# Gathers of table rows: each issued only once the second one before it has landed

## The chip, the core and the metric

The kernel runs on one core of a Trainium2 chip. The metric is the device time of one execution in microseconds (us), as the median of several runs. The core has a matrix engine (PE, with weight loads shown apart as PEld), a vector engine (DVE), a scalar engine (ACT), a general engine (POOL, called GpSimd in the program) and SyncE (SP), whose queue issues most plain DMAs. Each engine works through its own instructions in order, and they wait for one another through semaphores.

## What is computed

Four graph attention layers over 3327 nodes with 512 features; the graph is a random 0/1 matrix `adj` of 3327 x 3327 in which a row holds a few tens of ones at most. Cut to what matters, one layer is:

```python
h = jnp.maximum(_layernorm(x, axis=-1), 0.0)
Wh = h @ W                                   # split into heads: 8, 4, 1 and 8 in the four layers
e = leaky_relu(s_src[:, None] + s_dst[None, :], 0.2)     # s_src, s_dst: Wh dotted with two vectors
e = where(adj > 0, e, -inf)
x = x + softmax(e, axis=1) @ Wh              # in layers 1 and 2 with an elu around the product
```

In layer 0 and 1 every node is its own neighbour as well.

## The kernel before

The kernel makes use of how few neighbours a node has. In a first stage (`tile_gat_stack`) it reads `adj`, finds the column numbers of the ones in each row, sorts the nodes by their number of neighbours, and keeps for each of 26 tiles of 128 nodes a list of neighbour numbers, `CAPS[t]` of them (36 in the first tile, down to 11 in the last). If any row had too many ones, a dense kernel (`tile_gat_dense`) would run instead; it does not with these inputs.

The four layers are in `tile_gat_lists`. A node's features, already multiplied by the layer's weights, stand as one row of 528 floats (2112 bytes) in a table in HBM: `tabs[0]` and `tabs[1]` in turn, and `tabx` for layer 0, whose rows are double (features and the input `x` side by side). For a tile of 128 nodes, gather number k reads the row of each node's k-th neighbour: 128 rows, one in each partition, 270,336 bytes. The helper `gather` (L833) issues it on POOL as an indirect DMA: POOL writes the descriptors, the sixteen DMA engines move the rows. A node's own row needs no list and comes by a plain DMA on SP (L865), except in layer 0.

The work of a layer is a list of steps. A step is a group of up to `GROUP = 4` neighbours of one tile; tiles go from the last (shortest lists) to the first. Three methods of `Tile` make up a step. `fetch` issues the group's gathers into a buffer of `gpool`. `scored` adds the scores (DVE, L887), bends them and takes the exponential (ACT, L890). `group` multiplies the rows by the weights (DVE, L918) and lets PE sum them in PSUM (L923); in layer 2, with one head, DVE multiplies and adds in one operation (L911). When a tile's last group is done, a chain of pieces ends it: divisors, means, normalisation, transposes, product with the next layer's weights (L468), scaling (L475), and a store of the new row into the next table (L995).

The order on each engine is written out by hand (`tc.manual_schedule`): the loop over s issues the fetch of steps up to s + `LOOK`, then the scores of step s + 1, then the products of step s, then the pieces that `later` has put at this step. `LOOK` is 7, and `gpool` has seven buffers:

```python
                while fetched < min(len(steps), s + LOOK):
                    steps[fetched][0].fetch()
                    fetched += 1
```

A fetch waits for nothing but a free buffer and, at the start of a layer, for the rows of the last tile of the layer before.

Nodes with very long lists would need many gathers, so the first `DENSE[l]` tiles of layers 1 to 3 (1, 9 and 3 tiles) are done densely, as masked products over all nodes (`Wholes` in layer 2, `Several` in layers 1 and 3). Their rows come by plain DMAs on SP. The masks for them are made in layer 0: `Mask` gathers nine tiles of whole rows of `adj` (L1022), and `Ranked` gathers 26 pieces from `found` (L1063). These use the same helper `gather`.

POOL also does a few other things in the layers: reciprocal roots in layer 2 (L431), additions of weights in layer 2 (L1139), and the scatters of the finished rows to the output (L842, called by `scatter`), which are indirect DMAs but do not go through `gather`.

Of the kernel before, what the change touches and what calls it, by code (L numbers as in the profile page):

```python
# [33 lines left out]
FAR = -30000.0  # L34
ROW = 528
GROUP = 4
DENSE = [0, 1, 9, 3]
ND = max(DENSE)
ROUND = 1.5 * 2.0 ** 23
# [455 lines left out]
class Slots:  # L495
# [5 lines left out]
    class Part:  # L501
        def __init__(self, pool, name, blocks):
            self.blocks, c = [], 0
            for t0, t1 in blocks:
                k = CAPS[t0] if t0 >= min(DENSE) else 1
                self.blocks.append((t0, t1, k, c))
# [17 lines left out]
def tile_gat_stack(ctx: ExitStack, tc: tile.TileContext, x, adj, adjT, ws, avs, out):  # L524
# [266 lines left out]
    with cond.Else():  # L791
        tile_gat_lists(tc, x, adj, ws, avs, out, ident, half, slots, L, low, spare, tabx, tabs)
# [3 lines left out]
def tile_gat_lists(ctx: ExitStack, tc: tile.TileContext, x, adj, ws, avs, out, ident, half, slots, L, low, spare, tabx, tabs):  # L796
# [7 lines left out]
    nc = tc.nc  # L804
# [25 lines left out]
    nc.vector.memset(zero, 0.0)  # L830
    L, low, spare = [t.rearrange("p a b -> p (a b)") for t in (L, low, spare)]

    def gather(out_, table, which):  # L833
        nc.gpsimd.indirect_dma_start(out=out_, out_offset=None, in_=table,  # L834
                                     in_offset=bass.IndirectOffsetOnAxis(ap=which, axis=0))

    waiting = []

# [6 lines left out]
    class Tile:  # L845


        def __init__(self, l, t, W):
            self.l, self.t, self.W = l, t, W

            first = GROUP - 1 if l == 0 else GROUP
            self.k0 = [0] + list(range(first, CAPS[t], GROUP))
            self.own = first - 1 if l == 0 else 0
            self.groups = []

        def fetch(self):

            l, t = self.l, self.t
            i = len(self.groups)
            k0 = self.k0[i]  # L860
            n = (self.k0 + [CAPS[t]])[i + 1] - k0
            g = gpool.tile([P, GROUP, ROW], F32, name="g")
            for q in range(n):
                if l > 0 and k0 + q == 0:
                    nc.sync.dma_start(g[:, 0, :], tabs[l % 2][t * P:(t + 1) * P, :])  # L865
                elif l > 0:
                    gather(g[:, q, :], tabs[l % 2], slots(t, k0 + q))
                elif k0 + q == self.own:
                    gather(g[:, q:q + 2, :].rearrange("p q n -> p (q n)"), tabx, slots(t, 0))
                else:  # L870
                    gather(g[:, q, :], tabx.rearrange("r (s n) -> (r s) n", s=2),
                           slots(t, k0 + q + (k0 == 0), twice=True))
            self.groups.append((k0, n, g))

        def scored(self, i):
# [4 lines left out]
            if i == 0:  # L880
# [4 lines left out]
                nc.vector.tensor_copy(self.s, g[:, n, F:F + H] if self.l == 0 else g[:, 0, F // 2:F // 2 + H])  # L885
            z = small.tile([P, GROUP, 8], F32, name="z")[:, :n, :H]
            nc.vector.tensor_tensor(z, g[:, :n, ROW - 8:ROW - 8 + H],  # L887
# [9 lines left out]
        def group(self, i):  # L897


            H, K, wt = HEADS[self.l], CAPS[self.t], self.wt  # L900
            D = F // H
            k0, n, g = self.groups[i]
            if H == 1:
                for q in range(n):
                    v = g[:, q, :].rearrange("p (s m) -> p s m", s=2)[:, :, :F // 2]
                    acc = self.po.rearrange("p (s m) -> p s m", s=2)
                    w = wt[:, k0 + q, 0:1]
                    if k0 + q == 0:
                        nc.vector.tensor_scalar(acc, v, w, None, OP.mult)
                    else:  # L910
                        nc.vector.scalar_tensor_tensor(acc, v, w, acc, OP.mult, OP.add)  # L911
                return
            m = pools["m"].tile([P, GROUP, F], F32, name="m")
            for q in range(n):
                v = g[:, q, :].rearrange("p (s m) -> p s m", s=2)[:, :, :F // 2]

                out_ = self.po if k0 + q == 0 else m[:, q, :]
                nc.vector.tensor_tensor(out_.rearrange("p (s h d) -> p s h d", s=2, d=D),  # L918
                                        v.rearrange("p s (h d) -> p s h d", d=D),
                                        wt[:, k0 + q, :H].rearrange("p (s h) -> p s h", s=2)  # L920
                                        .unsqueeze(3).to_broadcast([P, 2, H // 2, D]), OP.mult)
            for q in range(k0 == 0, n):
                nc.tensor.matmul(self.po, ident, m[:, q, :], start=False, stop=(k0 + q == K - 1),  # L923
                                 skip_group_check=True)
# [89 lines left out]
    class Mask:  # L1014
# [12 lines left out]
        def group(self, i):  # L1027
            self.m = pools["m"].tile([P, GROUP, F], F32, name="m").rearrange("p q n -> p (q n)").bitcast(BF16)[:, :NP]
            nc.scalar.activation(self.m, self.a, AF.Copy)
# [310 lines left out]
    at = {}  # L1340
# [11 lines left out]
    for l in range(NL):  # L1352
# [3 lines left out]
        with ExitStack() as c2:  # L1356
            def pool(name, bufs, **kw):
                return c2.enter_context(tc.tile_pool(name=f"{name}{l}", bufs=bufs, **kw))
# [10 lines left out]
            else:  # L1369
                pools.update(m=pool("mpool", 3))  # L1370
                pools.update(p=pool("ps_p", 1 if DENSE[l] else 2, **psum))
                if DENSE[l]:
                    pools.update(w=pool("ps_w", l // 3 + 1, **psum), r=pool("ps_r", 1, **psum))
                    if DENSE[l] > 1:
                        pools.update(e=pool("epool", 1))
                    wholes = Several(l, DENSE[l], W)
                    pw = pools["p"].tile([P, BANK], F32, name="pw")
# [91 lines left out]
```

## Time and profile before

| what | value |
|---|---|
| median of three runs | 2429.07 us (2425.39 to 2435.29) |
| span of the profiled execution | 2971.7 us |
| first gather of layer 0 issued | 273.7 us |
| stretch of gathers in layer 0, 1, 2, 3 | 777, 690, 419, 629 us |
| gathers through the helper | 1511 |
| busy share of PE, DVE, POOL, ACT | 74%, 65%, 58%, 31% |
| POOL's time for one gather (issue) | 0.95 us |
| DMA: bytes moved, rate over the span | 594.21 MB, 200 GB/s |
| share of 16 DMA engines: software queue, SP's queue | 49.8%, 16.4% |

The profile comes from one execution, and that execution is longer than the runs: its span, from the first instruction to the last, is 2971.7 us, against a median of 2429.07 us. The profile gives no time of that execution other than its span. A busy time is the time in which an engine worked. In a row of waits the engine and line that waited stand ahead of the arrow, and what released them behind it. A gather's row on POOL shows the time in which POOL wrote descriptors; when the rows are in place is told by a semaphore, and can be read from what waits for it and from the records of single DMA packets.

### The profile page before, as it was taken

What the parts mean: (1) busy time and instruction counts of PE and PEld (TensorE: products, weight loads), DVE (VectorE), ACT (ScalarE), POOL (GpSimd) and SP (SyncE); (2) the same over time, 40 slices, a digit from 0 to 9 for tenths busy, and PEclk for the clock granted to TensorE, in tenths of its full rate; (3) what the DMA queues carried; (4) which work ended last, traced back from release to release, by engine and by line L of the source; (5) the groups of instructions that cost most, each with busy time, mean ns of one, the idle gap of its engine ahead of it and who ended that gap; (6) DMA issues with size and microseconds to landing.
All of it is one profiled execution on the core that took longest, in us unless ns stands there. A gap on an engine that the chain in (4) does not pass through costs nothing.

```text
span 2971.7 us, 27155 instructions
## 1 busy us (share of the span) xinstructions
PE 2211.9 (74%) x7082; PEld 1246.1 (42%) x7082; DVE 1923.1 (65%) x4968; ACT 934.6 (31%) x2502; POOL 1731.4 (58%) x1717
## 2 busy tenths in 40 slices
PE   4777677776777764767777877588696688878887
PEld 2564233343433332434444444244354454545443
DVE  7987666655565533656665665598888366666665
ACT  5872122322221111322222322244333333323330
POOL 7885455565566635544556562676664556555653
PEclk9988888888898887988888898799898898989888
DMA  6885576786676756755667673787785566656663
GB/s 230 325 291 161 165 228 200 211 254 207 195 225 197 199 130 200 200 157 174 187 190 210 179 209 92 234 255 240 241 246 153 168 193 204 185 170 198 195 189 111
DMA packets 260731, 594.21 MB, mean 200 GB/s; under 512 B 103699, under 2 KB 121107, under 8 KB 256214
## 3 DMA queue, kind: packets, MB, share of 16 engines
q0 software_dynamic: 124368, 432.13, 49.8%
q1 hardware_dynamic: 132454, 153.45, 16.4%
q10 hardware_dynamic: 3744, 6.82, 0.7%
q8 instruction: 57, 0.93, 0.1%
q14 instruction: 108, 0.88, 0.1%
HBM read 542.60 MB, written 49.65 MB: 199 GB/s over the span
## 4 chain that ended last, share of the span: by engine, by line
PE 24%; DVE 18%; issue 14%; another core or an unknown queue 8%; ACT 5%; POOL 3%; DMA 2%; SPq 0%; DVEq 0%; POOLq 0%; ACTq 0%
PE bank L923 16%; DVE m L918 6%; PE pv L468 4%; PE whole L1301 3%; DVE bank L911 3%; POOL g L834 3%; ACT r L1267 1%; DVE z L889 1%; DVE z L887 1%; DVE x L961 1%; PE whole L1153 1%; DMA g<-tab,idxb 1%; DVE em L1126 1%; DVE q L438 1%
## 5 line engine op out<-in xcount | busy, mean ns | idle before, releaser
L923 PE MATMUL bank<-m,ident 128*128 128x512 f32 x2414 | 1232.2, 659 | 335.9 <-DVE m L918 197.3
L918 DVE TENSOR_TENSOR m<-g,pw 128x512 f32<-128x512 f32 x1207 | 752.5, 682 | 384.1 <-ACT pw L890 209.2
L834 POOL DMA_INDIRECT g<-tab,idxb x712 | 678.8, 953 | 482.0 <-issue 197.1
L923 PEld LDWEIGHTS bank<-m,ident 128*128 128x128 f32 x2414 | 488.8, 211 | 942.1 <-issue 582.4
L468 PE MATMUL pv<-w,hT 128*128 128x264 f32 x1664 | 434.9, 416 | 87.8 <-ACT hT L457 61.8
L834 POOL DMA_INDIRECT g<-tabx,twiceb x342 | 324.8, 950 | 230.7 <-issue 147.7
L834 POOL DMA_INDIRECT g<-tab,idxa x297 | 283.7, 955 | 248.4 <-issue 83.9
L468 PEld LDWEIGHTS pv<-w,hT 128*128 128x128 f32 x1664 | 334.1, 205 | 190.3 <-ACT hT L457 68.7
L890 ACT ACTIVATE pw<-z 128x32 f32<-128x32 f32 (+4 forms) x356 | 67.8, 191 | 850.7 <-DVE z L889 484.2
L1153 PE MATMUL whole<-ve,em 128*128 128x512 f32 x468 | 229.4, 642 | 54.1 <-issue 22.9
L1301 PE MATMUL whole<-L,room 128*128 128x130 f32 x1248 | 173.3, 290 | 59.9 <-issue 59.5
L1301 PEld LDWEIGHTS whole<-L,room 128*128 128x128 f32 x1248 | 164.7, 202 | 91.4 <-issue 89.7
L694 POOL TENSOR_TENSOR key<-a,keys 128x3328 int32<-128x3328 int32 (+1 forms) x29 | 189.3, 6530 | 16.3 <-DVE cand L703 11.8
L911 DVE SCALAR_TENSOR_TENSOR bank<-g,L,bank 128x512 f32<-128x512 f32 x243 | 183.3, 754 | 11.1 <-remote 2.0
L1153 PEld LDWEIGHTS whole<-ve,em 128*128 128x128 f32 x468 | 94.0, 206 | 167.4 <-issue 124.5
L834 POOL DMA_INDIRECT g<-tabx,twicea x99 | 94.7, 956 | 104.1 <-issue 51.1
L450 PE MATMUL pt<-ident,xn 128*128 128x128 f32 x416 | 70.8, 298 | 104.7 <-ACT xn L969 60.8
L703 DVE MAX8 cand<-key 128x8 f32<-128x208 int32 x416 | 144.3, 365 | 0.1
L475 ACT ACTIVATE v<-pv,rstd 128x528 f32<-128x528 f32 x78 | 54.2, 694 | 274.4 <-remote 126.5
L1267 ACT ACTIVATE r<-low,L 128x384 f32<-128x384 f32 x208 | 121.2, 583 | 16.9 <-remote 9.5
L918 DVE TENSOR_TENSOR bank<-g,pw 128x512 f32<-128x512 f32 x74 | 51.5, 696 | 100.7 <-ACT pw L890 69.2
L450 PEld LDWEIGHTS pt<-ident,xn 128*128 128x128 f32 x416 | 54.7, 153 | 144.4 <-ACT xn L969 69.1
(180 smaller groups left out, 2195.7 us busy)
## 6 DMA issues: line engine op xcount, KB each, us to landing
a<-in_adj SPq DMA_DIRECT2D x25, 1664.0 KB
tab<-v SPq DMA_DIRECT2D x78, 264.0 KB
ve<-tab SPq DMA_DIRECT2D x78, 264.0 KB
g<-tab SPq DMA_DIRECT2D x65, 264.0 KB
tabx<-vx SPq DMA_DIRECT2D x26, 528.0 KB
g<-tab,idxb POOLq DMA_INDIRECT x712
low<-tab SPq DMA_DIRECT2D x52, 132.0 KB
spare<-tab SPq DMA_DIRECT2D x52, 132.0 KB
```

Source lines behind the costliest of these rows:

```text
L450: nc.tensor.transpose(pt[:, k, :], xn[:, k * P:(k + 1) * P], ident)
L468: nc.tensor.matmul(pv[:, s, :HF + 8], hT[:, k, :], W.w[:, k, s, :], start=(k == 0), stop=(k == KC - 1))
L694: nc.gpsimd.tensor_tensor(key[:, c:c + quarter], a[:, c:c + quarter], keys[:, c:c + quarter], OP.mult)
L703: nc.vector.max(cand[:, g * 8:(g + 1) * 8], key[:, g * SEG:(g + 1) * SEG])
L834: nc.gpsimd.indirect_dma_start(out=out_, out_offset=None, in_=table, in_offset=bass.IndirectOffsetOnAxis(ap=which, axis=0))
L890: nc.scalar.activation(self.wt[:, k0:k0 + n, :H], z, AF.Exp)
L911: nc.vector.scalar_tensor_tensor(acc, v, w, acc, OP.mult, OP.add)
L918: nc.vector.tensor_tensor(out_.rearrange("p (s h d) -> p s h d", s=2, d=D), v.rearrange("p s (h d) -> p s h d", d=D), wt[:, k0 + q, :H].re ...
L923: nc.tensor.matmul(self.po, ident, m[:, q, :], start=False, stop=(k0 + q == K - 1), skip_group_check=True)
L1153: nc.tensor.matmul(tl.po.rearrange("p (s m) -> p s m", s=2), e[:, q * P:(q + 1) * P], v.rearrange("p (s m) -> p s m", s=2)[:, :, :F // 2], ...
L1267: nc.scalar.activation(self.r[:, h, :], self.a[:, g, :], AF.Relu, bias=-1.0, scale=self.b[:, j, g:g + 1])
L1301: nc.tensor.matmul(dst, e[:, h, q * P:(q + 1) * P], mov, start=False, stop=(j == NT - 1), skip_group_check=True)
```

## The change

The helper keeps a list of the gathers issued last, two at most. When it issues a gather and two are on the list, the new gather is made dependent on the older of the two, in the sense that the older one's data has landed. So gather n waits for gather n-2, in the order of issue, across groups, tiles and layers, and for the gathers of `Mask` and `Ranked` too. The scatters (L842) are not in the list.

```diff
+FLYING = 2
...
+    flying = []
+
     def gather(out_, table, which):
-        nc.gpsimd.indirect_dma_start(out=out_, out_offset=None, in_=table,
-                                     in_offset=bass.IndirectOffsetOnAxis(ap=which, axis=0))
+        made = nc.gpsimd.indirect_dma_start(out=out_, out_offset=None, in_=table,
+                                            in_offset=bass.IndirectOffsetOnAxis(ap=which, axis=0))
+        if len(flying) == FLYING:
+            tc.add_manual_dep(made.ins, flying.pop(0).name,
+                              mybir.DependencyInfo(mybir.DependencyClass.Sync, mybir.DependencyReason.DATA),
+                              reason="few gathers at a time")
+        flying.append(made.ins)
```

## The prediction

> **What bounds the kernel now.** I read the page first, for the span and the shares of the engines.
>
> ```profile
> span 2971.7 us, 27155 instructions
> PE 2211.9 (74%) x7082; PEld 1246.1 (42%) x7082; DVE 1923.1 (65%) x4968; ACT 934.6 (31%) x2502; POOL 1731.4 (58%) x1717
> ```
>
> No engine is full. The page's chain of work that ended last goes to PE (24%), DVE (18%) and "issue" (14%): the four layers are paced by the reading side of each group (scores on DVE and ACT, products on DVE, sums on PE), with many small waits between those engines. Next I cut the span at the layers and asked for the instructions of L834 alone, which are the gathers. Columns: stretch, its length, busy POOL time with the number of gathers, granted TensorE clock, DMA share, GB/s.
>
> ```profile
> 273.00:1050.00 777.00, 459.33 (x483) 0.87 0.71 209
> 1117.00:1807.00 690.00, 385.12 (x406) 0.86 0.66 188
> 1854.00:2273.00 419.00, 235.59 (x243) 0.88 0.79 239
> 2313.00:2942.00 629.00, 341.81 (x360) 0.89 0.65 187
> ```
>
> One gather is issued per 777/483 = 1.61, 690/406 = 1.70, 419/243 = 1.72 and 629/360 = 1.75 us. These four numbers are what the changed kernel's pace has to be held against. They sum to 2515 us for 1492 gathers; the list building ahead (273 us), three layer changes (67, 47 and 40 us) and the end (30 us) make up the span.
>
> Then the waits of POOL, and those of DVE on gathers (who, for what, us in total, times, longest):
>
> ```profile
> POOL g L834 <- issue: 487.5, 1295, 16.3
> POOL g L834 <- DVE m L918: 219.9, 58, 11.4
> POOL g L834 <- DMA tab<-v: 82.8, 3, 47.7
> DVE z L887 <- DMA g<-tab,idxa: 56.2, 6, 16.8
> ```
>
> POOL runs ahead until the seven buffers of `gpool` are full and then stands until DVE frees one. DVE waited for a gather six times here, all at starts of layers. So gathers are off the critical path today, with a lead: from the trace's packet records a group's last gather lands a median of 22 us before its scores are read (layer 1: 24 us).
>
> Last, the start of layer 1, where the lead is zero and the time from issue to reader can be read directly (start, duration, engine, line):
>
> ```profile
> 1117.31 0.95 POOL L834 DMA_INDIRECT g<-tab,idxa  x1 [25.83 <-DMA tab<-v]
> 1118.56 0.95 POOL L834 DMA_INDIRECT g<-tab,idxa  x1 [0.31 <-issue]
> 1119.82 0.95 POOL L834 DMA_INDIRECT g<-tab,idxa  x1 [0.30 <-issue]
> ...
> 1123.63 0.17 DVE L887 TENSOR_TENSOR z<-g,pw 128x16 f32<-128x16 f32 x1 [15.96 <-DMA g<-tab,idxa]
> 1124.82 0.95 POOL L834 DMA_INDIRECT g<-tab,idxa  x1 [0.30 <-issue]
> ...
> 1128.58 0.94 POOL L834 DMA_INDIRECT g<-tab,idxa  x1 [0.30 <-issue]
> 1129.19 0.17 DVE L887 TENSOR_TENSOR z<-g,pw 128x16 f32<-128x16 f32 x1 [3.57 <-DMA g<-tab,idxa]
> ```
>
> Back to back, gathers start 1.25 us apart. The first group's third gather, issued at 1119.82, is read at 1123.63: 3.81 us. The second group's last, issued at 1124.82, is read at 1129.19: 4.37 us. Three more gathers were issued meanwhile.
>
> **Issue to landing, from the packet records.** Each gather ends with sixteen 4-byte packets on the software queue; I took the last of each sixteen. Over the 1450 gathers of single rows, from POOL's start to that packet's end: median 3.51 us, mean 3.68, 10% under 3.26, 10% over 4.23. By the number of gathers still in flight at issue the mean is 3.32 (none, 91), 3.57 (one, 151), 3.66 (two, 952), 3.83 (three, 220). The semaphore's last step follows the packet by 0.33 us (1121.89 to 1122.23, 1123.22 to 1123.55), and POOL starts a median of 0.26 us after a DVE semaphore that it waited for.
>
> **What the Trainium skill says.** "DMA: Bandwidth & Descriptors", section "Anatomy of one DMA — SWDGE (gpsimd) path", prices a DMA from GpSimd at 2.0 us plus bytes/436e3, most of the fixed part in the confirmation of the last byte. For 128 rows of 2112 bytes (270 KB) that estimate is 2.62 us; the trace shows 3.32 even with nothing else in flight, so I use the trace and keep 2.62 as a lower end. "Perfetto Trace Analysis", section "DMA Instruction — SWDGE (GPSIMD)", says that the profiler's end of such an instruction is the end of descriptor generation and not the landing. The trace agrees: 0.95 us of POOL time, first data packet 1.64 us after the start, landing two microseconds later still.
>
> **The change part by part.**
> *Removed: nothing.* Instructions, bytes and their order stay.
> *Added: one wait in every gather but the first two,* 1509 of the 1511. Gathers n and n-1 may be in flight and no more. In 83% of the single-row gathers (1198 of 1439 with the count known) two or more others were in flight at issue, so the wait binds nearly everywhere that POOL now runs at 1.25 us. Eight completion semaphores go round among POOL's DMAs, and a gather now often waits for the one eight before it; the new wait covers that one and can take its place, so I price its instruction at nothing; if that cover is gone, 1509 sequencer waits of 43 ns (such rows stand on POOL's queue) add 65 us of POOL time, mostly within the idle that the landing leaves.
> *The new pace.* Gather n starts at the landing of n-2, plus 0.33 us, plus 0.26. The landing lies between 3.14 us (median with none in flight) and 3.66 us (two in flight). A pair thus takes 3.73 to 4.25 us; I take 3.9, or 1.95 us a gather, since one is in flight at issue but the DMA engines are less pressed. The rows above (3.81 and 4.37 to a DVE reader) lie in that range. Idle POOL between two starts rises from 0.30 to about 1.0 us.
> *Per layer,* against 1.61 to 1.75 us: layer 0, 483 x 1.95 = 942, plus nine gathers of adjacency rows (median 7.5 us to land, so 4 us more each, 35) and 26 double rows (4.5 us, so 1.2 each, 31): 1008, or +231. Layer 1, 406 x 1.95 = 792: +102. Layer 2, whose gathers land later (median 3.79 us): 243 x 2.1 = 510: +91. Layer 3, 360 x 1.95 = 702: +73. Together +497.
> *What comes back.* The reading side no longer trails by 22 us at a layer's end: 15 us at each of three changes and 10 at the end, -55. Waits of POOL for buffers (DVE m, 219.9 us) go; they are inside the stretches and not subtracted again. The 19 last gathers of ranked lists between 1050 and 1117 lie in the drain of layer 0.
> The sum in the profiled execution: 2971.7 + 497 - 55 = 3414 us, +15%.
> *Queued behind the waiting gather on POOL:* 26 reciprocal roots of layer 2 (L431, 0.61 us), 39 additions of masked weights (L1139, 1.01 us), the 26 final scatters (L842). ACT waits for the roots (L475), DVE for the additions (L1145). POOL now stands several steps behind DVE in program order, where before it was level, so these come later; but the reader cannot use the next group earlier either. I cost them at nothing inside the new pace; without that cover 65 of them a microsecond late each would be 65 us. SP's and ACT's queues are not touched.
>
> **From the profile to the runs.** The runs' median, 2429.07 us, is 0.817 of the span, and the profile does not show what is longer under it. If everything shrinks alike, 3414 becomes 2789. If the landing chain does not shrink at all, only list building and gaps do (about 400 us, by 18%): 3340. An issue-to-landing time made of transfers should shrink less than chains of small instructions, so the truth lies between; I forecast **3000 us**, +23%, a pair of about 3.4 us.
>
> **Rivals.**
> 1. *The landing is much quicker outside the profile and the lead hides most of it.* For: the skill's 2.62 us, with 0.3 for the wake, makes a pair of 2.9, or 1.46 a gather, where the runs need 0.817 x 1.69 = 1.38. Against: 3.32 us with nothing in flight. Price: 1492 x 0.08 = 120: about 2550 (2450 to 2650).
> 2. *No change.* The wait is satisfied by issue and not by landing, or a queue's order is taken for granted. Against: landings and issues have different semaphores here. Time 2429.
> 3. *Faster.* Fewer gathers at a time leave the DMA engines to SP's loads and stores. Place: the layer change, where POOL waits 82.8 us in three waits for `tab<-v`, and ACT's wait for "remote" at L475 (126.5 us). Price: a quarter of both, 52 us, times 0.82: about 2385. It decides only if a pair takes less than 2 x 1.38 = 2.76 us, so that the wait never holds the layer up; no landing in the trace is that short with its wake.
>
> **Chances and range.** Gathers pace the layers (2650 to 3340): 0.80. Rival 1: 0.11. No change: 0.03. Faster: 0.02. Longer than 3340, if the landing does not shrink and the roots and additions are late too: 0.04. The range 2620 to 3340 leaves out under 0.2. The measurement tells 0.5% (12 us) from no change. Faster 0.02, same 0.03, slower 0.95.
>
> **What would show it.** After: POOL's idle before a gather names the gathers' own DMAs, about 1.0 us each over some 1400 gathers, and the wait for DVE m L918 is nearly gone; DVE's wait for gathers (L887) rises from tens to hundreds of us; one gather per 1.9 to 2.1 us in all four layers, layer 0 growing most; the lead falls from 22 us to a few; in flight at issue never over one. Wrong: if POOL still runs at 1.25 us (rival 2), if landings come at 2.6 us (rival 1), or if the pair is right but layers move by different amounts, because a reader is late for another cause.

## The result

The changed kernel takes 3486.95 us (median of four runs, 3482.8 to 3490.85) against 2430.45 us before: a ratio of 1.4347 (95% interval 1.4322 to 1.4372), 1057 us more. It is slower, as forecast, but by almost twice as much as forecast (+570 us), and outside the range.

The profile that the prediction was made from caught a disturbed execution of the kernel before, 22% longer than any run; a new profile of the same kernel (the first experiment below) spans 2431.3 us, as the runs do. The kernel before is therefore shown here again, from that new profile.

From the page, the kernel before (new profile) and then the changed kernel, with the shares of its chain of work that ended last:

```profile
span 2431.3 us, 27155 instructions
PE 2056.3 (85%) x7082; PEld 1185.0 (49%) x7082; DVE 1924.5 (79%) x4968; ACT 930.0 (38%) x2502; POOL 1728.6 (71%) x1717
```

```profile
span 3489.1 us, 27142 instructions
PE 2385.8 (68%) x7082; PEld 1288.3 (37%) x7082; DVE 1929.1 (55%) x4968; ACT 932.8 (27%) x2502; POOL 1726.6 (49%) x1717
DMA 63%; issue 11%; DVE 9%; POOL 4%; ACT 2%; PE 2%; POOLq 0%; DVEq 0%; ACTq 0%
```

The work is the same: DVE 1924 and 1929 us, POOL 1729 and 1727 us. (PE's busy time grows by 330 us; its granted clock is 0.84, where it was 0.945.) In the last line 63% of the changed kernel's span is DMA. The new profile of before gives nothing to hold against it, since its chain can be followed back only to 1657 us, over the last third of the span.

Cut at the layers, gathers alone, the kernel before (new profile) and then the changed kernel. Columns: stretch, length, busy POOL time with the number of gathers, granted TensorE clock, DMA share, GB/s:

```profile
274.00:890.00 616.00, 458.10 (x483) 0.98 0.87 264
925.00:1451.00 526.00, 384.01 (x406) 0.97 0.83 248
1483.00:1894.00 411.00, 235.00 (x243) 0.89 0.80 244
1935.00:2411.00 476.00, 340.32 (x360) 0.98 0.83 247
```

```profile
273.00:1288.00 1015.00, 458.24 (x483) 0.82 0.59 161
1322.00:2147.00 825.00, 383.95 (x406) 0.85 0.59 160
2178.00:2702.00 524.00, 234.88 (x243) 0.82 0.67 193
2732.00:3469.00 737.00, 340.85 (x360) 0.87 0.58 159
```

The stretches sum to 2029 us before and 3101 us after: 1072 us more, where the spans differ by 1058: the whole difference lies in the stretches. Per gather it is 1.28, 1.30, 1.69 and 1.32 us before, and 2.10, 2.03, 2.16 and 2.05 us after. The changed kernel has nearly one pace in all four layers. Its waits of POOL and DVE for gathers, the seven costliest, and what is left of POOL's wait for a free buffer (who, for what, us, times, longest):

```profile
POOL g L837 <- DMA g<-tab,idxb: 531.2, 490, 3.1
DVE z L895 <- DMA g<-tab,idxb: 442.7, 129, 7.1
DVE z L895 <- DMA g<-tabx,twiceb: 342.4, 80, 8.7
POOL g L837 <- DMA g<-tabx,twiceb: 292.5, 252, 3.6
POOL g L837 <- DMA g<-tab,idxa: 232.9, 207, 3.6
DVE z L895 <- DMA g<-tab,idxa: 216.1, 55, 32.3
POOL g L837 <- DMA g<-tabx,twicea: 80.6, 76, 2.0
POOL g L837 <- DVE m L926: 45.5, 29, 2.1
```

POOL now waits for gathers over a thousand times, and behind it DVE waits for them too. In the new profile of before, DVE waited 67 and 46 us for gathers, and POOL 34.4 us for `DVE m`: the 219.9 us that it waited there in the first profile were those of the disturbed execution.

### The profile page after: what moved, and what is told of

It is laid out like the page before. It is cut to its first block, busy times and chain, and to the rows that moved or that the text cites. A ratio compares the mean times of both kernels' runs of the same rounds, so it can differ in the third digit from the quotient of the medians.

```text
span 3489.1 us, 27142 instructions
## 1 busy us (share of the span) xinstructions
PE 2385.8 (68%) x7082; PEld 1288.3 (37%) x7082; DVE 1929.1 (55%) x4968; ACT 932.8 (27%) x2502; POOL 1726.6 (49%) x1717
## 4 chain that ended last, share of the span: by engine, by line
DMA 63%; issue 11%; DVE 9%; POOL 4%; ACT 2%; PE 2%; POOLq 0%; DVEq 0%; ACTq 0%
DMA g<-tab,idxb 27%; DMA g<-tabx,twiceb 16%; DMA g<-tab,idxa 11%; DMA g<-tabx,twicea 4%; DVE m L926 3%; POOL g L837 3%; DMA low<-in_adj,idxb 2%; DVE bank L919 1%; PE pv L469 1%; PE bank L931 1%; POOL parts L1147 1%; DVE z L895 1%; DMA g<-tabx,idxb 1%; DVE z L897 1%; DVE x L969 0%
## 5 line engine op out<-in xcount | busy, mean ns | idle before, releaser
L931 PE MATMUL bank<-m,ident 128*128 128x512 f32 x2414 | 1412.5, 737 | 723.9 <-DVE m L926 723.7
L931 PEld LDWEIGHTS bank<-m,ident 128*128 128x128 f32 x2414 | 535.2, 234 | 1452.6 <-DVE m L926 998.3
L895 DVE TENSOR_TENSOR z<-g,pw 128x32 f32<-128x32 f32 (+4 forms) x356 | 63.5, 178 | 1043.2 <-DMA g<-tab,idxb 442.7
L1161 PE MATMUL whole<-ve,em 128*128 128x512 f32 x468 | 242.6, 673 | 110.9 <-DVE em L1134 103.2
L1309 PEld LDWEIGHTS whole<-L,room 128*128 128x128 f32 x1248 | 148.7, 191 | 27.1 <-issue 23.1
L1309 PE MATMUL whole<-L,room 128*128 128x130 f32 x1248 | 148.6, 274 | 0.0
L1127 ACT ACTIVATE r<-low,mc,b 128x384 f32<-128x384 f32 x78 | 52.6, 675 | 242.4 <-DVE em L1134 205.7
```

The lines of the kernel that those rows point to most:

```text
L895: nc.vector.tensor_tensor(z, g[:, :n, ROW - 8:ROW - 8 + H], self.s.unsqueeze(1).to_broadcast([P, n, H]), OP.add)
L1161: nc.tensor.matmul(tl.po.rearrange("p (s m) -> p s m", s=2), e[:, q * P:(q + 1) * P], v.rearrange("p (s m) -> p s m", s=2)[:, :, :F // 2], ...
L1309: nc.tensor.matmul(dst, e[:, h, q * P:(q + 1) * P], mov, start=False, stop=(j == NT - 1), skip_group_check=True)
```

## The experiments

My theory: two gathers can start in the time from a gather's issue to POOL's knowing that it has landed, and that pace now sets the layers. Rivals: the waiting instructions themselves cost (whatever they wait for); POOL's other work and its order hold layers back; what is lost depends on something of the reading side.

**1. The kernel before, profiled again.** No edit. The changed kernel's profile (3489.1 us) equals its runs; the first profile of before did not, so the base had to be looked at first.

> The kernel before, unchanged, profiled once more. It asks why the first profile spans 2971.7 us where the runs take 2430 us, while the changed kernel's profile (3489.1 us) equals its runs. Theory 'odd execution': the first profile caught an execution that is not like the runs; a new one spans 2430 us, its layers pace at about 1.38 us a gather. Theory 'the profiler slows it': a new profile spans about 2970 us again, since the profiler costs time where engines are dense with small instructions, and the changed kernel hides that cost in its waits.

Measured: 2430.35 us in the runs, span 2431.3 us, granted clock 0.945 against 0.873 in the first profile. So "odd execution" holds: the profiler does not slow this kernel, and in each of the twelve profiles taken after the first, the span is within 2 us of the time of that same execution. None of the 43 timed runs of the kernel before took over 2435.3 us. The first profile does carry a sign of it. 77 waits, 500 us together, end there with a releaser named "remote", one that the profile doesn't show, though the program runs on one core; 49 of them (357 us) are ACT's. No other profile here has a single one. The costliest:

```profile
ACT v L475 <- remote: 126.5, 11, 19.8
```

What held ACT up stays open. POOL in the middle of layer 1, in the new profile (start, duration, engine, line):

```profile
1100.18 0.94 POOL L834 DMA_INDIRECT g<-tab,idxb  x1 [0.30 <-issue]
1101.42 0.95 POOL L834 DMA_INDIRECT g<-tab,idxb  x1 [0.30 <-issue]
1102.67 0.95 POOL L834 DMA_INDIRECT g<-tab,idxb  x1 [0.30 <-issue]
1105.58 0.94 POOL L834 DMA_INDIRECT g<-tab,idxb  x1 [1.96 <-DVE m L918]
1106.83 0.94 POOL L834 DMA_INDIRECT g<-tab,idxb  x1 [0.30 <-issue]
```

Over the whole kernel 92% of the intervals between two gathers are under 1.3 us, and the median is 1.251. In layers 0, 1 and 3 the kernel before thus runs close to the rate at which POOL can issue gathers at all. The lead of a group's last landing over its reader is a median of 3.7 us in layer 0, 10.3, 20.8 and 9.7 us in the others, not 22 us.

**2 to 5. More gathers in flight, or fewer.** The edit is the constant alone, in the changed kernel:

```diff
-FLYING = 2
+FLYING = 3
```

and in the same way 4, 6 and 1.

> FLYING = 3 in the changed kernel: a gather waits for the third one before it. Theory 'landing pace': the pace is (issue to landing 3.5 + 0.6 us) / 3 = 1.37 us a gather plus some 0.1 for uneven spacing, against about 1.4 in the runs of before; 2440 to 2620 us. Rival 'the waits themselves cost' (1509 instructions more to wait on, about 0.7 us each): as slow as FLYING = 2, near 3480 us.

> FLYING = 4 in the changed kernel. Theory 'landing pace': four gathers 1.25 us apart take 5.0 us, longer than the 4.1 us from issue to landing and wake, so the wait is over before it is reached: 2425 to 2450 us, no change. Rival 'the waits themselves cost': near 3480 us.

> FLYING = 6 in the changed kernel: the waits are there, but six gathers take 7.5 us to issue and nearly all have landed by then, adjacency rows (7 us) apart. Theory 'landing pace': what FLYING = 4 lost (103 us) goes with the tail of slow landings: 2425 to 2445 us. Rival 'the waits themselves cost': the loss of FLYING = 4 stays, 2500 us or more.

> FLYING = 1 in the changed kernel: each gather waits for the one just before it. Theory 'landing pace': one gather per issue-to-landing time alone (about 3.1 us) plus 0.6 us, and half a microsecond more where the wait stands in an instruction of its own: 1511 x 3.75 = 5670, plus list building, layer changes and the slower gathers of masks and double rows (470): about 6130 us, 5900 to 6300. Rival 'what costs is leaving the DMA queue empty now and then, not the time of a round trip': less than twice the loss of FLYING = 2, under 4550 us.

Measured, with what the traces' packet records give (mean from issue to the last packet of a single-row gather, and the pace of layer 1):

| FLYING | us | ratio (95% interval) | issue to landing, us | layer 1, us per gather |
|---|---|---|---|---|
| no wait | 2430 | 1 | 3.85 | 1.30 |
| 6 | 2446.30 | 1.0066 (1.0047 to 1.0086) | 3.77 | 1.30 |
| 4 | 2533.53 | 1.0433 (1.0407 to 1.0459) | 3.79 | 1.33 |
| 3 | 2787.35 | 1.1475 (1.1431 to 1.1519) | 3.64 | 1.54 |
| 2 | 3486.95 | 1.4347 (1.4322 to 1.4372) | 3.31 | 2.03 |
| 1 | 6208.51 | 2.5563 (2.5512 to 2.5615) | 3.12 | 3.84 |

The order and size follow the round trip. With one in flight, 3.12 + 0.6 = 3.7 us against 3.84 measured; with two, (3.31 + 0.6)/2 = 1.96 against 2.03; with three, (3.64 + 0.6)/3 = 1.41 against 1.54. For 2 and for 6 nearly the same number of gathers have a waiting instruction of the sequencer (a wait that stands by itself in POOL's stream) ahead of them (421 and 407), and 6 costs 16 us: "the waits themselves cost" falls. So does "an empty queue": one in flight loses more than three times what two lose.

My two misses here are FLYING = 3 and 4, where I expected 2440 to 2620 and no change; FLYING = 6 ended 1 us above its 2425 to 2445. The base is the likely reason. At FLYING = 4 the issue of four gathers (5.0 us) leaves some 0.6 us over a mean round trip of 4.4, so each slow landing shows, and a kernel that already issues gathers as fast as POOL can has little lead to pay from. POOL's longest waits for gathers with FLYING = 4:

```profile
POOL g L837 <- DMA g<-tab,idxb: 45.7, 103, 1.8
POOL g L837 <- DMA low<-in_adj,idxb: 25.8, 6, 5.1
POOL g L837 <- DMA g<-tabx,twiceb: 22.1, 37, 1.6
POOL g L837 <- DMA g<-tab,idxa: 20.4, 48, 1.5
```

All of POOL's waits for gathers sum to 139 us there and to 28 us in the new profile of before (91 waits, none over 0.3 us, which is the usual gap): 111 us more, for a time that is 103 us longer.

**6. The additions of layer 2 off POOL.** The prediction had costed at nothing what stands behind a waiting gather on POOL. It had also said that the lead would fall to a few us; in layers 0, 1 and 3 of the changed kernel it is 0.5 us (median), so that the reading side takes each group as it lands and holds nothing up there, but in layer 2 the gathers still land 20.6 us ahead of their readers, and DVE waits for POOL's additions:

```profile
DVE parts L1153 <- POOL parts L1147: 95.1, 17, 9.6
```

```diff
-            nc.gpsimd.tensor_tensor(self.part(p, i // 2)[:, 1 + i % 2, :], two[:, 0, :], two[:, 1, :], OP.add)
+            nc.vector.tensor_tensor(self.part(p, i // 2)[:, 1 + i % 2, :], two[:, 0, :], two[:, 1, :], OP.add)
```

> The changed kernel (FLYING = 2) with the 39 additions of masked weights in layer 2 on DVE and not on POOL, so that they no longer stand behind waiting gathers. Layer 2's gathers still run 20 us ahead of their readers in the changed kernel, unlike those of the other layers, and DVE waits there 95 us for these additions. Theory 'order on POOL holds layer 2': the stretch of layer 2 shortens from 522 us towards its landing pace, 243 x 1.95 = 474 us, and the whole by 30 to 60 us: about 3440 us. Rival 'landing pace everywhere': the whole stays within 15 us of 3487, or rises by the 20 us of work put on DVE.

Measured: 3479.42 us (1.4329, 1.4288 to 1.4370), not told apart from the changed kernel. The lead in layer 2 fell from 20.6 to 6.2 us and the stretch by about 11 us. "Order on POOL holds layer 2", which stood for 30 to 60 us, falls: the lead there was no slack. The readers stood behind because POOL, whose additions they need, is some steps behind in its own order (that its roots make up the rest of the lead is not shown); but POOL issues gathers at 2.16 and 2.11 us there with and without the additions, and that pace sets the layer.

**7 to 9. What POOL's own time is worth, before and after.** A memset that nothing reads goes ahead of every gather, once and then twice in the kernel before, once in the changed kernel:

```diff
+    idle = spool.tile([P, 64], F32, name="idle", bufs=1)
+
     def gather(out_, table, which):
+        nc.gpsimd.memset(idle, 0.0)
```

> The kernel before, with one memset of 128 x 64 on POOL ahead of every gather (1511 of them; nothing reads it). Theory 'before is paced by POOL's issue of gathers' (1.30 to 1.32 us a gather in layers 0, 1 and 3 of the new profile against 1.25 back to back): each memset adds 0.15 to 0.35 us to the pace of 1249 gathers in those layers, 190 to 440 us in all: 2620 to 2870 us. Rival 'before is paced by PE and DVE' (PE is busy 85%): the memsets fill idle POOL time, under 30 us.

> The kernel before with two memsets of 128 x 64 on POOL ahead of every gather. One memset raised the back-to-back pace from 1.251 to 1.282 us only, as it fell into the gap between two gathers, and the time by 39 us, which is 0.031 x 1249. A second one doesn't fit into the gap and takes 0.17 us plus a gap of its own, so the pace rises to 1.45 to 1.6 us. Theory 'before is paced by POOL's issue': 1249 x (0.20 to 0.35), 250 to 440 us more than before: 2680 to 2870 us. Rival 'paced by PE and DVE with a lead': under 80 us more.

> The changed kernel with the same memset ahead of every gather. Theory 'landing pace': POOL stands idle about 0.8 us ahead of a gather, the memset falls into it: 3480 to 3530 us. Rival 'POOL's own instructions pace the changed kernel too': 190 to 440 us longer.

Measured: before with one memset 2467.20 us (1.0158, 1.0141 to 1.0175); before with two 2882.00 us (1.186, 1.184 to 1.1879); the changed kernel with one 3489.42 us (1.437, 1.4346 to 1.4394), unchanged.

The first expectation was wrong in its size (39 us more lies between the theory's 190 and the rival's 30), and the trace shows why. POOL, the kernel before with one memset:

```profile
1202.66 0.95 POOL L837 DMA_INDIRECT g<-tab,idxb  x1 [0.16 <-issue]
1203.62 0.17 POOL L836 MEMSET idle<- 128x64 f32 x1
1203.95 0.95 POOL L837 DMA_INDIRECT g<-tab,idxb  x1 [0.16 <-issue]
```

The memset (0.17 us) falls into the 0.30 us between two gathers; the median interval rises from 1.251 to 1.282. Times the 1249 gathers of layers 0, 1 and 3 that is 0.031 x 1249 = 39 us, and the time rose by 39 us. With two memsets (12 us above the expected range) the median is 1.475, and about a quarter of the intervals in those layers, 331 of them, where a gather has waits in an instruction of their own, are near 1.9: 0.224 x 1249 = 280 us and 0.43 x 331 = 142 us. Layer 2's stretch grows by 34 us, which makes 456 together; measured 451. So in layers 0, 1 and 3 the kernel before pays for every bit of POOL time per gather: it was paced by POOL's issue, not by the reading side. The changed kernel pays nothing, since POOL idles ahead of its gathers.

**10. Where the wait stands.** POOL in layer 1 of the changed kernel:

```profile
1359.90 0.94 POOL L837 DMA_INDIRECT g<-tab,idxa  x1 [2.45 <-DMA g<-tab,idxa]
1361.15 0.95 POOL L837 DMA_INDIRECT g<-tab,idxa  x1 [0.30 <-issue]
1363.53 0.95 POOL L837 DMA_INDIRECT g<-tab,idxa  x1 [1.44 <-DMA g<-tab,idxa]
1365.09 0.95 POOL L837 DMA_INDIRECT g<-tab,idxa  x1 [0.61 <-DMA g<-tab,idxa]
1367.78 0.95 POOL L837 DMA_INDIRECT g<-tab,idxa  x1 [1.74 <-DMA g<-tab,idxa]
```

The mean of a pair is 4.23 us over the whole kernel, while issue to landing is 3.34 over all gathers; the start follows the landing by 0.89 us on average and not by 0.59. Part of that is no pace: without the first two gathers of layers 1 to 3, which wait for the layer before, the pair is 4.16 us and the start follows by 0.81. By kind: the gathers that carry the landing wait themselves start a median of 0.60 us after the last packet. About 409 gathers (mostly a group's first, which waits for a free buffer too) have an instruction of the sequencer ahead of them that takes the landing wait, and start 1.08 us after it. To take the second wait away, a memset ahead of each group takes the waits for the buffer:

```diff
-            g = gpool.tile([P, GROUP, ROW], F32, name="g")
+            g = gpool.tile([P, GROUP * ROW + 8], F32, name="g")
+            nc.gpsimd.memset(g[:, GROUP * ROW:], 0.0)
+            g = g[:, :GROUP * ROW].rearrange("p (q n) -> p q n", q=GROUP)
```

> The changed kernel with a memset of 128 x 8 of the group's buffer (eight columns more, which nothing reads) ahead of each group's first gather, so that the memset takes the waits for the buffer, and the gather has its landing wait alone. In the changed kernel a gather whose landing wait stands in an instruction of its own starts 1.08 us after the landing, the others 0.60 us. Theory 'the doubled wait costs': about 409 gathers start 0.48 us sooner, half of it in the pace as two chains alternate: 98 us less, 60 to 200 us less if the spacing gets more even too: 3290 to 3430 us. Rival 'only uneven spacing': 3470 us or more.

Measured: 3373.89 us (1.3898, 1.3874 to 1.3921), 113 us less than the changed kernel, with 428 memsets more. Starts follow landings by 0.60 us (median) nearly everywhere, and the mean pair is 4.07 us, or 3.99 without the first two gathers of layers 1 to 3. The doubled wait costs about what it was held to cost (98 us).

**11. The slow gathers.** The nine gathers of adjacency rows and the 26 of ranked lists neither wait nor count:

```diff
-    def gather(out_, table, which):
+    def gather(out_, table, which, limited=True):
...
+        if not limited:
+            return
         if len(flying) == FLYING:
...
-            gather(self.a, adj, slots(self.t, 0))
+            gather(self.a, adj, slots(self.t, 0), limited=False)
...
-            gather(self.rows, found, slots(self.j, 0))
+            gather(self.rows, found, slots(self.j, 0), limited=False)
```

> The changed kernel, but the nine gathers of adjacency rows and the 26 of ranked lists neither wait nor count. The prediction priced the nine at 35 us; layer 0 takes 2.18 us a gather against 2.03 to 2.05 in layers 1 and 3, 60 us over its 467, and the ranked lists at its end issue faster. Theory: 40 to 80 us less than 3487. Rival 'they hide behind their neighbours': under 15 us less.

Measured: 3432.51 us (1.412, 1.4097 to 1.4144), 54 us less than the changed kernel. Of these, 27 us are in layer 0, whose 467 gathers of table rows fall from 2.18 to 2.12 us each (adjacency rows and some ranked lists stand between them); layers 1 and 3 move by 0.03 us a gather or less.

No version here beats the kernel before. Its bound points at fewer or cheaper issues on POOL, which was not tried. What it could give is not shown either: the memsets tell what more POOL time costs, not what less is worth, and PE is busy for 542 of 616 us in layer 0 of the kernel before, 478 of 526 in layer 1 and 456 of 476 in layer 3.

## Why the prediction was wrong

Of the 487 us between the forecast (3000) and the measurement (3487), the step from the profile to the runs lost 414 (3414 to 3000), and the sum ahead of it 73 (3487 - 3414).

**From the profile to the runs: this step failed.** It read the ratio of median to span (0.817) as something that the profile does to the program, and put the changed kernel between a full share of it (2789) and none in the layers (3340). The right factor was 1: the changed kernel's profile spans 3489 us and its runs take 3487. Even the upper end shortened list building and gaps by 18%, some 70 us that were never there: the first gather starts at 274 us in the disturbed, the new and the changed kernel's profile alike. With that step left out, the prediction's own sum, 3414, lies 2% below the measurement. The argument that a time made of transfers shrinks less than chains of small instructions pointed the right way, but the forecast still went more than half of the way down from 3340 to 2789, and no number of the profile stood behind that.

**What bounds the kernel before: wrong, and the ground for that step.** The prediction read from the chain and the waits that the reading side paces the layers, and from the packets that gathers run 22 us ahead. That fits the disturbed execution alone. Undisturbed, three of four layers run at 1.28 to 1.32 us a gather, against 1.25 back to back, and experiments 7 and 8 show that POOL's time per gather is what they pay for. Its base of 1.61 to 1.75 us a gather also made the loss look small: its four stretches of 3012 us are 497 us more than the disturbed execution's, but 983 more than the 2029 us of the undisturbed one. A sign was there: 2430 us less the 273 us of list building and some 150 us of changes and end leaves 1.35 us for each of 1492 gathers, close to the 1.25 us of the issue. The prediction used this figure (1.38) only to price a rival.

**The pace of a pair: right in mechanism, 3% too small in the sum.** The stretches were forecast at 1008, 792, 510 and 702 us, and took 1015, 825, 524 and 737: 3101 and not 3012, 89 us more. With 0.33 and 0.26 us for the wake, 3.9 us leave 3.31 for the landing, which is the changed kernel's mean for single rows; that the prediction chose just this value from its 3.14 to 3.66 was in part luck. What was mis-sized is the wake of the gathers with two kinds of wait: 1.08 us and not 0.59 for about 409 of them, whose wait was priced "at nothing" as one that takes an old one's place. Doing without it brings 113 us, which covers the 89. The slow gathers were priced at 66 us in layer 0 with the double rows; freeing the masks and ranked lists, without the double rows, brings 54 us, half of it in layer 0. Uneven spacing of the two chains (a gather doesn't follow the one before it by less than 1.25 us) adds little by the trace of the changed kernel: 221 gathers start less than 1.3 us after the one before, on average 0.91 us after their landing in place of 0.60, and half of that over 221 gathers is 34 us.

**The sum in the profiled execution: 3414 us, measured 3489.** It is right within 2.2%, in the stretches for the right reason: 1.95 us for each gather is a new time, not an addition to the old one, so the disturbed base falls out. Outside the stretches it was luck. The prediction had 457 us there in the disturbed execution and took off 55 as "what comes back", which leaves 402. The undisturbed kernel has 402 us there to begin with (2431 - 2029), and the changed one 388 (3489 - 3101): 14 us came back, not 55, since the readers of the undisturbed kernel had not trailed by 22 us in most layers.

**What stands behind a waiting gather, costed at nothing: right.** Experiment 6 moved the additions away and gained nothing that can be told from no change. For the roots this was not tested.

**Rivals.** 1 (landings quicker outside the profile) falls: issue to landing is 3.12 us even when only one gather is in flight, in an undisturbed execution, so the 2.62 us worked out as an estimate from the Trainium skill's "DMA: Bandwidth & Descriptors", section "Anatomy of one DMA — SWDGE (gpsimd) path", are too short for these gathers. 2 (no change) falls: one gather is in flight at issue in 1455 of 1537 cases, scatters counted. 3 (faster, DMA engines freed) falls: POOL's wait for the rows of the last table (`tab<-v`) did drop, from 53.2 to 41.5 us, and 12 us is all. The 126.5 us of "remote" that it counted on were the disturbance's and stand in no other profile.

## What to carry to other kernels

A limit of k transfers in flight sets a pace of (issue to landing + wake)/k, as long as that is longer than one issue. Work it out and hold it against the pace that the kernel has now, issue cost included; where the loop already runs at the issue rate, even a limit that is met on average (FLYING = 4) can cost, 103 us here. And where a profile's span and the median of the runs differ by a fifth, the profile may simply not be of an execution like the runs: look for waits without a releaser, test its reading against the runs' own pace, and carry over times in us that do not depend on the base, not a ratio.

## What the runs showed of the hardware

The time from issue to landing of a 270 KB gather falls with the limit on gathers in flight, from a mean of 3.85 us with no limit to 3.12 us with one; with one, a tenth of them still take under 2.97 us and half over 3.06. POOL's descriptor writing, 0.95 us, is within it. Without any limit, POOL issues these gathers 1.25 us apart, 0.95 us busy and 0.30 us between. A POOL instruction starts 0.60 us after the last packet of a DMA that it waits for itself, and 1.08 us after it when an instruction of the sequencer takes that wait first. A memset of 128 x 64 on POOL between two gathers cost 0.03 us of pace, since it fits into the 0.30 us that lie between two gathers anyway; a second one cost 0.19 us more, and about 0.6 us where a gather has a wait in an instruction of its own.
